# One-core graph-and-expert network: the last stage's weight ring takes over six shared buffers, and the first two experts are ranked from two banks

## The chip, the cores and the metric

The kernel runs on one core of one Trainium2 chip. The metric is the device time in microseconds (us) of one execution, from the first to the last instruction with what lies around them. Three runs of the kernel before gave a median of 4235.73 us (4232.37 to 4238.52). All instants below are us from the start of the profiled span.

## The reference, cut to what matters

The network works on 512 nodes of 768 features (`x`, float32) and passes through four groups of layers, each a graph layer, a mixing layer and a feed-forward layer. All stages but the last are the same in both kernels. The last one, a mixture of experts, normalises `x` (mean and variance over the features), and then:

- scores each token for 16 experts: sigmoid of `x` times a gate matrix;
- each expert takes the 64 tokens with the highest scores (ties go to the token with the lower number), which needs the rank of each token's score among the 512 scores of that expert;
- a chosen token goes through its expert: `Wd(silu(Wg x) * (Wu x))` with 3,072 hidden units, is multiplied by its score and added to the token's row;
- a shared expert of 1,536 hidden units, of the same form, works on all tokens and is added too.

The output is `x` with these sums added, 512 x 768 float32.

## The kernel before, in words

A layer called Tile builds the program: each engine (PE, which multiplies matrices; VectorE, "DVE" in the profile; ACT, the scalar engine; GpSimd, "POOL"; SP, which issues transfers) has a queue of its own, in an order that the layer's scheduler decides. `issue_after(i)` makes the instructions under it stand behind the instruction `i` in that order. Waits between engines and for buffers come by themselves from what the instructions read and write. Where ACT and VectorE read the same bank of the accumulation memory (a tile `ps`, 128 x 512 float32; there are eight), the layer makes them wait for each other.

**Stage before the last.** `last_two` multiplies `x` with the weights of the mixing layer (`m3_wqkv`, `m3_wp`) beside a graph layer. Its weights, like those of all earlier stages, go through the pool `wp` of six buffers of 1,152 KB (`w`, `wk`, `wr`, line 257; SP issues the transfers). It ends, token block by token block (four of 128), with `norm1` (L401 to L405: statistics and reciprocal on VectorE, the root on ACT, the scaling on VectorE) and writes each normalised block to a table `f3_there` in memory outside the core. `to_fm` with a cut (L354, L249, L251) transposes the first three blocks into the tile `xnT`, which has features on the partitions, with copies alternately on VectorE and ACT, and then the last block, in two triples of chunks.

**The last stage, `ffn3`.** On entry it closes the stack `cw`, which frees the pools `wp` and `rowp`, and opens a ring of 13 buffers, `f3_w`. Its head is a chain:

- the gate (L341), two half copies (L1717 on VectorE, L1718 on ACT), a turn back to tokens (L333), the sigmoid (L1720);
- `first_rank` for the experts 0 and 1: PE spreads the expert's 512 scores over all partitions into one bank (four transposes, L354). For each of the four token blocks, ACT takes the sign of the difference to every other score and adds the signs up (L1735), and VectorE counts the equal scores with weights of one half (L1738). Both read the bank;
- L1897 and L1898 make ranks of these; `choose(0)` compares the ranks with 0 to 63 and gives one-hot rows `oh` (L1766); `fetch(0)` multiplies them by the token numbers on PE, sums and casts these on VectorE (L1777, L1779), and GpSimd gathers the 128 rows from `f3_there` (L1781); `turn(0)` transposes them (L354) to `xg`;
- beside this, by hand, PE gets `shared(0, 0)` behind the last sign, and `shared(0, 1)` behind the product of `fetch`. `shared(u, b)` is half of one of 12 units of the shared expert: six matmuls of 128 x 512 in the program (twelve in the trace, since float32 takes two), then Silu on ACT (L1827) or a product on VectorE (L1829). Its weights `sw` come by GpSimd's queue (L1820), six buffers.

Then come 64 steps: eight pairs of experts, eight slices of the hidden units each. A step is `up` (two experts side by side, 64 columns each: L1851; Silu L1854, product L1855) and `down` (L1867). Its weights are six ring buffers: two `f3_Wg`, two `f3_Wu`, two `f3_Wd`. The `up` of the next step is placed ahead of the `down` of this one. A table `beside` says what else goes along with each step: the ranks, choices and gathers of the next pair (`rank`, L1752 and L1755), `way` (the products `os` of one-hot rows and scores, L1798, turned), `back` (the sum into `x`, L410), and the rest of the 12 shared units, cut into pieces and spread evenly over the first 60 steps. The last block's sums are followed by the stores of the output.

Of the kernel before, what the change touches and what calls it, by code (L numbers as in the profile page):

```python
# [1 line left out]

# [1 line left out]

# [7 lines left out]
BF16 = mybir.dt.bfloat16  # L12
# [3 lines left out]
OP = mybir.AluOpType  # L16
# [4 lines left out]
P = 128  # L21
# [148 lines left out]
class Net:  # L170
    def __init__(self, ctx, tc, dram, at, out):
        self.tc, self.nc, self.d, self.at, self.out = tc, tc.nc, dram, at, out
        nc = self.nc
        self.cw = ExitStack()
        self.wp = self.cw.enter_context(tc.tile_pool(name="wp", bufs=6, side="right"))
        self.keep = ctx.enter_context(tc.tile_pool(name="keep", bufs=1))
        self.small = ctx.enter_context(tc.tile_pool(name="small", bufs=4))
        self.rowp = self.cw.enter_context(tc.tile_pool(name="rowp", bufs=2, side="right"))
        self.pp = ctx.enter_context(tc.tile_pool(name="pp", bufs=8, space=PSUM))
        self.dp = ctx.enter_context(tc.tile_pool(name="dp", bufs=1, space=DRAM))  # L180
        self.turn = 0
# [36 lines left out]
        nc.gpsimd.memset(self.big0, -BIG)  # L218
        self.wq1 = keep.tile([P, KC, 32], F32, name="wq1")
        self.gate = None  # L220
        self.lower = keep.tile([P, P], BF16, name="lower")

        self.number = keep.tile([P, NT, 2], BF16, name="number")
        for t in range(NT):
            nc.gpsimd.memset(self.number[:, t, 1:2], float(t * P))
# [37 lines left out]
            self.before -= 1  # L263
        return t

    def wk(self, ap):

        return self.w(ap).rearrange("p (k n) -> p k n", k=KC)

    def wr(self, ap, pool=None):  # L270

# [81 lines left out]
        k = in_.shape[0]  # L353
        self.nc.tensor.transpose(out, in_, self.ident[:k, :k])  # L354

    def to_fm(self, x, out, cut=0):

        if cut:
            ps = [self.ps() for _ in range(KC)]
            for t in range(cut // P):  # L360
                for f in range(KC):
                    self.tr(ps[f][:, t * P : (t + 1) * P], x[:, t, f * P : (f + 1) * P])
            for f in range(KC):
                self.copy(out[:, f, :cut], ps[f][:, :cut])
            for f in range(0, KC, 3):
                p = self.ps()
                for k in range(3):
                    self.tr(p[:, k * P : (k + 1) * P], x[:, NT - 1, (f + k) * P : (f + k + 1) * P])
                self.copy(out[:, f : f + 3, cut:], p[:, :HW].rearrange("p (k n) -> p k n", k=3))
            return  # L370
        ps = [self.ps() for _ in range(KC)]
        for t in range(NT):
            for f in range(KC):
                self.tr(ps[f][:, t * P : (t + 1) * P], x[:, t, f * P : (f + 1) * P])
        for f in range(KC):
            self.copy(out[:, f, :], ps[f])

    def to_tm(self, xT, done):

# [14 lines left out]
    def norm1(self, x, out, t):  # L394
# [10 lines left out]
        nc.vector.tensor_scalar(out[:, t, :], x[:, t, :], mv[:, 0:1], r, OP.subtract, OP.mult)  # L405

    def add_x(self, t, nb, p):

# [1272 lines left out]
        yield  # L1681
        add(*after)

    def ffn3(self, xnT, gate, there):

# [4 lines left out]
        with ExitStack() as c:  # L1690
# [1 line left out]
            one = c.enter_context(tc.tile_pool(name="f3_one", bufs=1))  # L1692
            sp = c.enter_context(tc.tile_pool(name="f3_s", bufs=6))

            self.cw.close()
            self.wp = c.enter_context(tc.tile_pool(name="f3_w", bufs=13))

            first = self.small.tile([P, 1], F32, name="r3")
            with self.tc.issue_after(self.root):
                nc.scalar.activation(first, self.eps, AF.Sigmoid)  # L1700
            io = one.tile([P, P], F32, name="io")
            nc.gpsimd.iota(io, pattern=[[1, P]], base=0, channel_multiplier=0, allow_small_or_imprecise_dtypes=True)
# [26 lines left out]
            def first_rank(e):  # L1729
                p = self.ps()  # L1730
                for t in range(NT):
                    self.tr(p[:, t * P : (t + 1) * P], sc[:, t, e : e + 1].to_broadcast([P, P]))
                for t in range(NT):
                    junk = one.tile([P, N], BF16, name="sign")
                    i = nc.scalar.activation(junk, p, AF.Sign, scale=BIGGER, bias=low[:, t, e : e + 1],  # L1735
                                             accum_out=signs[:, t, e : e + 1])
                    junk = one.tile([P, N], BF16, name="junk")
                    nc.vector.scalar_tensor_tensor(junk, p, sc[:, t, e : e + 1], side[:, (3 - t) * P : (7 - t) * P],  # L1738
                                                   OP.is_equal, OP.mult, accum_out=sides[:, t, e : e + 1])
                return i  # L1740

            def rank(e):

# [25 lines left out]
            rows = {}  # L1769

            def fetch(q):

# [6 lines left out]
                nc.vector.tensor_copy(who, sums)  # L1779
                rows[q] = two.tile([P, D], F32, name="rows", bufs=1)  # L1780
                nc.gpsimd.indirect_dma_start(out=rows[q], out_offset=None, in_=there,  # L1781
                                             in_offset=bass.IndirectOffsetOnAxis(ap=who, axis=0))
                return i

            def turn(q):
# [8 lines left out]
            def way(q):  # L1794

                oh = chosen[q][0]
                os = two.tile([P, NT, 2, CAP], F32, name="os", bufs=1)
                nc.vector.tensor_mul(os, oh, sc[:, :, 2 * q : 2 * q + 2, None].to_broadcast([P, NT, 2, CAP]))  # L1798
                ways[q] = two.tile([P, N], F32, name="ohT")
                p = self.ps()  # L1800
                for t in range(NT):
# [10 lines left out]

            hs = {}

            def shared(u, b):
                if b == 0:
                    hs[u] = [two.tile([P, N], F32, name="hs")]
                    for n in ("f3_sg", "f3_su", "f3_sd"):
# [2 lines left out]
                        hs[u].append(w)  # L1821
                p = self.ps()
                w = hs[u][1 + b].rearrange("p (k m) -> p k m", k=KC)
                i = self.acc(p, [(w[:, k, :], xnT[:, k, :]) for k in range(KC)])
                h = hs[u][0]
                if b == 0:
                    nc.scalar.activation(h, p, AF.Silu)  # L1827
                else:
                    nc.vector.tensor_mul(h, h, p)  # L1829
# [7 lines left out]


            def up_w(q, n):
                return [[self.wk(d[w][2 * q + a, n]) for a in range(2)] for w in ("f3_Wg", "f3_Wu")]  # L1840

            def down_w(q, n):
                return [self.wr(d["f3_Wd"][2 * q + a, n]) for a in range(2)]

            def up(q, n, ws):
                xg = chosen[q][1]
# [85 lines left out]
def tile_net(ctx, tc, dram, at, out, only=ALL):  # L1932
# [56 lines left out]
    with tc.tile_pool(name="f3_x", bufs=1) as last:  # L1989
# [4 lines left out]
        with tc.tile_pool(name="f3_n", bufs=1) as p2:  # L1994
# [1 line left out]
            net.moe("f2", AF.Silu, xn)  # L1996
            there = net.last_two(xn, xnT, xn)

            net.to_fm(xn, xnT, (NT - 1) * P)
        net.ffn3(xnT, gate, there)  # L2000


def build(arrays, at, only=ALL):
# [20 lines left out]
```

## Time and profile before

| what | us |
|---|---|
| median of three runs | 4235.73 |
| the profiled execution | 4235.37 |
| its span, first to last instruction | 4233.6 |
| PE busy in the span | 4092.9 (97%) |
| VectorE, ACT, GpSimd busy | 1295.3, 664.4, 274.2 |
| first transfer of the last stage's ring issued | 3111.48 |
| first matmul of an expert | 3143.44 |
| end of the last matmul of an expert | 4224.0 |

The granted clock of PE is 0.989 over the span (1 is full). The three kinds of ring weights are 384 transfers of 1,152 KB, and take a median of 14.6 to 14.7 us from issue to landing, since several are under way at once. In the profile's rows a line such as L1735 stands for the instruction's source line, `sign<-ps,low` for what it writes and reads, and a bracket for the idle time of its engine ahead of it and what ended it. The ends of matmuls are modelled; their starts are not.

### The profile page before, as it was taken

The page shows a single profiled execution, that of the slowest core. Times are in us where ns is not written, and L with a number is a line of the kernel's source. Part 1 is how long each engine was busy: PE and PEld are TensorE (multiplying, and loading weights), DVE is VectorE, ACT ScalarE, POOL GpSimd, SP SyncE. Part 2 cuts the span into 40 slices and gives each one's busy share as a digit, 9 for nine tenths or more (in the row PEclk, how much of TensorE's full clock was granted, in tenths as well). Part 3 has the DMA queues.
Part 4 walks back from the last instruction along what each step waited for, and adds up shares of the span by engine and source line. Part 5 has one row for each costly group of instructions (what it writes and reads, how often), then busy time and mean ns, then how long its engine had stood idle before and what let it go on. Part 6 is the DMA issues. An engine that isn't in the chain of part 4 may idle for free. (4 is left out here: it accounts for less than half of the span.)

```text
span 4233.6 us, 40102 instructions
## 1 busy us (share of the span) xinstructions
PE 4092.9 (97%) x16356; PEld 2094.4 (49%) x16356; DVE 1295.3 (31%) x3096; ACT 664.4 (16%) x1258; POOL 274.2 (6%) x325
## 2 busy tenths in 40 slices
PE   9989999999989999999999999989989999999999
PEld 3434555554455566755644444445654444444444
DVE  8871111112432135613220101034751222122211
ACT  1221200001312223511200000012620000000000
POOL 1120000001022010000000000021110000000000
PEclk9999999999999999999999999989999999999999
DMA  3111011111047112211211111064069999999998
GB/s 111 53 64 56 23 45 67 68 56 54 18 178 291 42 56 72 109 45 56 98 44 57 55 56 53 4 237 155 12 282 427 427 427 426 427 427 427 420 425 366
DMA packets 99549, 710.90 MB, mean 168 GB/s; under 512 B 12608, under 2 KB 12945, under 8 KB 29985
## 3 DMA queue, kind: packets, MB, share of 16 engines
q1 hardware_dynamic: 78064, 601.20, 35.2%
q0 software_dynamic: 16816, 95.80, 6.0%
q10 hardware_dynamic: 4480, 11.28, 0.7%
q8 instruction: 132, 2.16, 0.2%
q14 instruction: 57, 0.46, 0.0%
HBM read 685.68 MB, written 22.54 MB: 167 GB/s over the span
## 5 line engine op out<-in xcount | busy, mean ns | idle before, releaser
L1851 PE MATMUL ps<-w,xg 128*64 128x384 f32 x3072 | 567.1, 489 | 0.3 <-DVE xg L249 0.3
L1851 PEld LDWEIGHTS ps<-w,xg 128*64 128x64 f32 x3072 | 235.8, 137 | 287.0 <-issue 257.5
L1473 PE MATMUL ps<-aT,w 128*128 128x512 f32 x864 | 372.3, 592 | 0.0
L1867 PE MATMUL ps<-w,hT 128*64 128x384 f32 x1536 | 319.4, 490 | 3.4 <-ACT hT L251 1.9
L333 PE MATMUL ps<-xnT,w 128*128 128x512 f32 (+1 forms) x732 | 321.5, 596 | 0.2 <-ACT xnT L251 0.2
L1473 PEld LDWEIGHTS ps<-aT,w 128*128 128x128 f32 x864 | 164.4, 190 | 203.4 <-issue 202.1
L333 PE MATMUL ps<-w,xnT 128*128 128x384 f32 x672 | 221.6, 487 | 0.2 <-DVE xnT L249 0.2
L333 PEld LDWEIGHTS ps<-xnT,w 128*128 128x128 f32 (+1 forms) x732 | 134.3, 184 | 174.7 <-issue 171.1
L1867 PEld LDWEIGHTS ps<-w,hT 128*64 128x64 f32 x1536 | 131.8, 137 | 166.7 <-issue 137.1
L410 DVE TENSOR_TENSOR x<-x,ps 128x384 f32<-128x384 f32 x224 | 123.5, 553 | 262.7 <-PE ps L333 192.7
L333 PE MATMUL ps<-C,parts 128*128 128x512 bf16 x864 | 188.6, 380 | 2.7 <-DVE inv L1495 2.7
L333 PE MATMUL ps<-w,hT 128*128 128x384 f32 x552 | 184.7, 490 | 3.9 <-ACTq L942 3.9
L514 PE MATMUL ps<-ohd,so 128*128 128x512 bf16 x816 | 184.1, 386 | 2.7 <-DVE so L511 2.7
L333 PEld LDWEIGHTS ps<-w,xnT 128*128 128x128 f32 x672 | 127.2, 190 | 88.4 <-issue 4.7
L1483 DVE TENSOR_TENSOR aT<-inv,ps 128x512 f32<-128x512 f32 x72 | 49.5, 687 | 365.6 <-PE ps L333 365.6
L1854 ACT ACTIVATE h<-ps 128x384 f32<-128x384 f32 x64 | 31.4, 490 | 781.5 <-PE ps L1851 781.5
L1855 DVE TENSOR_TENSOR h<-h,ps 128x384 f32<-128x384 f32 x64 | 35.4, 554 | 371.6 <-PE ps L1851 371.6
L333 PEld LDWEIGHTS ps<-w,hT 128*128 128x128 f32 x552 | 103.3, 190 | 81.2 <-ACT xbT L251 7.6
L333 PE MATMUL ps<-w,aT 128*128 128x384 f32 (+1 forms) x416 | 139.6, 486 | 0.5 <-DVE aT L249 0.4
L333 PE MATMUL ps<-xnT,sw 128*128 128x512 f32 x288 | 139.3, 615 | 0.0
L333 PEld LDWEIGHTS <-parts 128*128 128x128 bf16 x864 | 84.7, 98 | 108.1 <-issue 8.8
L514 PEld LDWEIGHTS <-so 128*128 128x128 bf16 x816 | 79.7, 99 | 107.6 <-DVE so L511 14.3
(511 smaller groups left out, 4826.7 us busy)
## 6 DMA issues: line engine op xcount, KB each, us to landing
w<-in_f_Wg_dram SPq DMA_DIRECT2D x128, 1152.0 KB, 14.6
w<-in_f_Wu_dram SPq DMA_DIRECT2D x128, 1152.0 KB, 14.7
w<-in_f_Wd_dram SPq DMA_DIRECT2D x128, 1152.0 KB, 14.6
w<-in_g_w_dram SPq DMA_DIRECT2D x54, 1152.0 KB, 5.1
w<-in_m_wqkv_dram SPq DMA_DIRECT2D x24, 1152.0 KB, 8.3
w<-in_g_t_dram SPq DMA_DIRECT2D x12, 1152.0 KB, 6.3
w<-in_m_wp_dram SPq DMA_DIRECT2D x8, 1152.0 KB, 5.2
ea<-in_edge_attr_dram SPq DMA_DIRECT2D x34, 256.0 KB, 2.7
```

What stands on the lines that cost most here:

```text
L333: i = self.nc.tensor.matmul(out, a, b, start=n == 0, stop=n == len(pairs) - 1)
L410: self.nc.vector.tensor_add(xs, xs, p)
L514: nc.tensor.matmul(p, so[:, n, t * P : (t + 1) * P], ohd[:, j, :], start=False, stop=j == (g + 1) * HJ - 1)
L1473: nc.tensor.matmul(outs[nb * 3 + f], w[:, k, f * P : (f + 1) * P], xT[:, k, :], start=first and k == 0, stop=last and k == KC - 1)
L1483: nc.vector.tensor_mul(aT[:, f, :], inv[:, r, :], p)
L1851: nc.tensor.matmul(p[a * 64 : a * 64 + 64, :HW], xg[:, k, a * CAP : (a + 1) * CAP], ws[b][a][:, k, :], start=k == 0, stop=k == KC - 1)
L1854: nc.scalar.activation(h, pg[:, :HW], AF.Silu)
L1855: nc.vector.tensor_mul(h, h, pu[:, :HW])
L1867: nc.tensor.matmul(po[nb][a * 64 : a * 64 + 64, :HW], hT[:, f * P + a * 64 : f * P + a * 64 + 64], wd[a][:, f, nb * HW : (nb + 1) * HW], s ...
```

## The change

- Pools: `rowp` gets a stack of its own. On entry, `ffn3` closes that stack only, keeps the six buffers of `wp`, and opens seven more (`f3_w`). The ring of the last stage goes through the six and then the seven, in turn.
- The copies into `xnT` for the last stage (`to_fm_last`): ACT takes the chunks 0, 1, 3 and 4 and the first triple of the last block, VectorE the chunks 2 and 5, issued behind the last scaling, and the second triple. The sigmoid's table is loaded behind ACT's last copy, not behind the last root.
- `first_ranks`: both experts' scores are spread, each in its own bank. ACT takes the signs of expert 0 while VectorE counts for expert 1; then they change over. Each engine has the same eight instructions as before.
- The product `os` of `way(q)` is issued behind the cast in `fetch(q)` (`casts[q]`).
- PE's order by hand: `shared(0, 0)`, the first three chunks of `shared(0, 1)`, the product of `fetch(0)`, the other three chunks, `shared(1, 0)`, and then `turn(0)`. The piece `shared(1, 0)` leaves the table `beside`.

```diff
-        self.rowp = self.cw.enter_context(tc.tile_pool(name="rowp", bufs=2, side="right"))
+        self.cr = ExitStack()
+        self.rowp = self.cr.enter_context(tc.tile_pool(name="rowp", bufs=2, side="right"))
...
+    def to_fm_last(self, x, out):
...
+        for f in (0, 1, 3, 4):
+            i = nc.scalar.copy(out[:, f, :cut], ps[f][:, :cut])
+        with self.tc.issue_after(self.scaled):
+            for f in (2, 5):
+                nc.vector.tensor_copy(out[:, f, :cut], ps[f][:, :cut])
...
+            if f:
+                nc.vector.tensor_copy(*at)
+            else:
+                with self.tc.issue_after(i.ins):
+                    i = nc.scalar.copy(*at)
+        return i.ins
...
-            self.cw.close()
-            self.wp = c.enter_context(tc.tile_pool(name="f3_w", bufs=13))
+            self.cr.close()
+            c.callback(self.cw.close)
+            more = c.enter_context(tc.tile_pool(name="f3_w", bufs=7))
+            self.taken = 0
+
+            def ring():
+                self.taken += 1
+                return self.wp if (self.taken - 1) % 13 < 6 else more
...
-            with self.tc.issue_after(self.root):
+            with self.tc.issue_after(turned):
                 nc.scalar.activation(first, self.eps, AF.Sigmoid)
...
+            def first_ranks():
+
+                ps = [self.ps() for _ in range(2)]
+                for e in range(2):
+                    for t in range(NT):
+                        self.tr(ps[e][:, t * P : (t + 1) * P], sc[:, t, e : e + 1].to_broadcast([P, P]))
+                for e in range(2):
+                    for t in range(NT):
+                        junk = one.tile([P, N], BF16, name="sign")
+                        i = nc.scalar.activation(junk, ps[e], AF.Sign, scale=BIGGER, bias=low[:, t, e : e + 1],
+                                                 accum_out=signs[:, t, e : e + 1])
+                    for t in range(NT):
+                        junk = one.tile([P, N], BF16, name="junk")
+                        j = nc.vector.scalar_tensor_tensor(
+                            junk, ps[1 - e], sc[:, t, 1 - e : 2 - e], side[:, (3 - t) * P : (7 - t) * P],
+                            OP.is_equal, OP.mult, accum_out=sides[:, t, 1 - e : 2 - e])
+                return i, j
...
-                nc.vector.tensor_mul(os, oh, sc[:, :, 2 * q : 2 * q + 2, None].to_broadcast([P, NT, 2, CAP]))
+                with tc.issue_after(casts[q]):
+                    nc.vector.tensor_mul(os, oh, sc[:, :, 2 * q : 2 * q + 2, None].to_broadcast([P, NT, 2, CAP]))
...
-                i = self.acc(p, [(w[:, k, :], xnT[:, k, :]) for k in range(KC)])
                 h = hs[u][0]
+                i = None
+                for k in range(KC):
+                    with tc.issue_after(i.ins) if i else nullcontext():
+                        i = nc.tensor.matmul(p, w[:, k, :], xnT[:, k, :], start=k == 0, stop=k == KC - 1)
+                    if between and k == KC // 2 - 1:
+                        with tc.issue_after(i.ins):
+                            i = between()
...
-                return [[self.wk(d[w][2 * q + a, n]) for a in range(2)] for w in ("f3_Wg", "f3_Wu")]
+                return [[self.wk(d[w][2 * q + a, n], ring()) for a in range(2)] for w in ("f3_Wg", "f3_Wu")]
...
-            rest = pieces[2:]
+            rest = pieces[2:4] + pieces[5:]
...
-            for e in range(2):
-                last = first_rank(e)
+            last, _ = first_ranks()
...
             with tc.issue_after(last.ins):
                 last = shared(0, 0)
             choose(0)
-
             with tc.issue_after(last.ins):
-                last = fetch(0)
+                last = shared(0, 1, lambda: fetch(0))
             with tc.issue_after(last.ins):
-                shared(0, 1)
+                shared(1, 0)
             turn(0)
```

More of the change, by code (lines that the diff above doesn't have):

```diff
@@ L1 @@
-from contextlib import ExitStack
+from contextlib import ExitStack, nullcontext
 import numpy as np
@@ L264, in w, with wk @@
         return t
-    def wk(self, ap):
-        return self.w(ap).rearrange("p (k n) -> p k n", k=KC)
+    def wk(self, ap, pool=None):
+        return self.w(ap, pool).rearrange("p (k n) -> p k n", k=KC)
     def wr(self, ap, pool=None):
@@ L354, in tr, with to_fm @@
         self.nc.tensor.transpose(out, in_, self.ident[:k, :k])
[L356 to L370, printed above, removed]
+    def to_fm(self, x, out):
         ps = [self.ps() for _ in range(KC)]
@@ L376, in to_fm @@
             self.copy(out[:, f, :], ps[f])
+    def to_fm_last(self, x, out):
+        nc, cut = self.nc, (NT - 1) * P
+        ps = [self.ps() for _ in range(KC)]
+        for t in range(NT - 1):
+            for f in range(KC):
+                self.tr(ps[f][:, t * P : (t + 1) * P], x[:, t, f * P : (f + 1) * P])
+        for f in (0, 1, 3, 4):
[3 more added lines that the diff above has]
+                nc.vector.tensor_copy(out[:, f, :cut], ps[f][:, :cut])
+        for f in range(0, KC, 3):
+            p = self.ps()
+            for k in range(3):
+                self.tr(p[:, k * P : (k + 1) * P], x[:, NT - 1, (f + k) * P : (f + k + 1) * P])
+            at = out[:, f : f + 3, cut:], p[:, :HW].rearrange("p (k n) -> p k n", k=3)
+            if f:
[4 more added lines that the diff above has]
+        return i.ins
     def to_tm(self, xT, done):
@@ L404, in norm1 @@
         nc.vector.reciprocal(r, r)
-        nc.vector.tensor_scalar(out[:, t, :], x[:, t, :], mv[:, 0:1], r, OP.subtract, OP.mult)
+        self.scaled = nc.vector.tensor_scalar(out[:, t, :], x[:, t, :], mv[:, 0:1], r, OP.subtract, OP.mult).ins
     def add_x(self, t, nb, p):
@@ L1682, in gnn3, with ffn3 @@
         add(*after)
-    def ffn3(self, xnT, gate, there):
+    def ffn3(self, xnT, gate, there, turned):
         nc, tc, d = self.nc, self.tc, self.d
@@ L1727, in ffn3 @@
             sides = one.tile([P, NT, 2], F32, name="sides")
[L1729 to L1740, printed above, removed]
+            def first_ranks():
[14 more added lines that the diff above has]
+                return i, j
             def rank(e):
@@ L1767, in choose @@
                                             above[:, t, 2 * q : 2 * q + 2, None].to_broadcast([P, 2, CAP]), OP.is_equal)
-            rows = {}
+            rows, casts = {}, {}
             def fetch(q):
@@ L1778, in fetch @@
                 who = two.tile([P, 1], I32, name="who")
-                nc.vector.tensor_copy(who, sums)
+                cast = nc.vector.tensor_copy(who, sums)
                 rows[q] = two.tile([P, D], F32, name="rows", bufs=1)
@@ L1782, in fetch @@
                                              in_offset=bass.IndirectOffsetOnAxis(ap=who, axis=0))
+                casts[q] = cast.ins
                 return i
@@ L1813, in ffn3, with shared @@
             hs = {}
-            def shared(u, b):
+            def shared(u, b, between=None):
                 if b == 0:
@@ L1839, in up_w @@
             def up_w(q, n):
-                return [[self.wk(d[w][2 * q + a, n]) for a in range(2)] for w in ("f3_Wg", "f3_Wu")]
+                return [[self.wk(d[w][2 * q + a, n], ring()) for a in range(2)] for w in ("f3_Wg", "f3_Wu")]
             def down_w(q, n):
-                return [self.wr(d["f3_Wd"][2 * q + a, n]) for a in range(2)]
+                return [self.wr(d["f3_Wd"][2 * q + a, n], ring()) for a in range(2)]
             def up(q, n, ws):
@@ L1997, in tile_net @@
             there = net.last_two(xn, xnT, xn)
-            net.to_fm(xn, xnT, (NT - 1) * P)
-        net.ffn3(xnT, gate, there)
+            turned = net.to_fm_last(xn, xnT)
+        net.ffn3(xnT, gate, there, turned)
 def build(arrays, at, only=ALL):
```

## The prediction

> **What bounds the kernel now.** The change touches only the last stage, so the first view is the table of busy time by stretch of that stage (columns: the stretch, its length, then busy us and instructions of PE, PE's weight loads, VectorE, ACT, GpSimd, then granted clock, DMA share, GB/s).
> ```profile
> 3100.00:3150.00 50.00, 39.41 (x165) 20.55 (x165) 17.76 (x46) 13.25 (x30) 5.60 (x11) 0.90 0.80 326
> ...
> 3300.00:3400.00 100.00, 100.00 (x487) 43.79 (x484) 16.99 (x41) 5.24 (x11) 3.16 (x5) 1.00 1.01 427
> ...
> 4100.00:4200.00 100.00, 99.38 (x531) 44.09 (x529) 15.68 (x28) 5.92 (x12) 0.00 (x0) 1.00 1.01 422
> ```
> From 3150 to the end PE and the DMA engines are both full: 427 GB/s in stretch after stretch, and PE without a hole. Only the 50 us at the stage's head have PE time to give. So I next split that head:
> ```profile
> 3126.00:3133.20 7.20, 0.00 (x0) 0.00 (x1) 4.41 (x14) 4.61 (x11) 0.54 (x1) 0.68 1.01 428
> 3133.20:3139.00 5.80, 5.74 (x10) 2.52 (x11) 1.45 (x6) 0.43 (x1) 1.04 (x1) 0.51 1.01 429
> ```
> PE stands still for 7.2 us while the first two experts are ranked, and then runs at half clock. The timeline says why the ranking is slow:
> ```profile
> 3126.07 0.69 ACT L1735 ACTIVATE sign<-ps,low 128x512 bf16<-128x512 f32 x1
> 3126.08 0.75 DVE L1738 SCALAR_TENSOR_TENSOR junk<-ps,sc,side 128x512 bf16<-128x512 f32 x1 [0.85 <-ACT sign L1735]
> ...
> 3126.94 0.75 DVE L1738 SCALAR_TENSOR_TENSOR junk<-ps,sc,side 128x512 bf16<-128x512 f32 x1
> ...
> 3127.73 0.69 ACT L1735 ACTIVATE sign<-ps,low 128x512 bf16<-128x512 f32 x1 [0.88 <-DVE junk L1738]
> ...
> 3128.54 0.75 DVE L1738 SCALAR_TENSOR_TENSOR junk<-ps,sc,side 128x512 bf16<-128x512 f32 x1 [0.84 <-ACT sign L1735]
> ```
> ACT and VectorE take turns on one bank (waits of 0.85 us at every step). Only at 3126.07, where one is in expert 0's bank and the other already in expert 1's, do they run at once, and neither gets longer. Last, the waits from 3160 to the end decide between PE and DMA:
> ```profile
> PEld ps L1867 <- DMA w<-in_f_Wg_dram: 10.4, 18, 0.8
> ...
> PEld ps L1851 <- DMA w<-in_f_Wd_dram: 7.5, 14, 0.8
> ```
> In 1,074 us PE is put down as waiting for weights for 18.7 us (0.8 for Wu), never over 0.8 at once; a gap of 0.6 to 0.8 also stands ("issue") at other changes between 64 and 128 columns, so hardly any of it is a real wait. Counting the weights' packets, a weight lands 12 to 24 us before its first matmul in mid-stage. The lead melts only in steps 61 to 63, where PE has no other work (12.2 us a step), and the last pair of Wd lands 2.0 us before its use. So PE sets the end, with the DMA 2 us behind it.
>
> **The change, part by part.** Sums are against the profiled execution: span 4233.6, own time 4235.37 (1.8 lie around the span), 0.4 under the median 4235.73.
>
> Transposed copies. In the trace before, the reciprocal waits behind a copy on VectorE: ACT's root ends at 3113.16, the scaling starts at 3113.86; without the copy it starts 0.24 us after the root (as at 3097.01 to 3097.25), 0.46 earlier. The sigmoid table (1.28 us) no longer stands ahead of ACT's copies; it moves into ACT's wait for the gate. VectorE keeps three copies of 0.55 behind the scaling and ends about where it did (3115.7), but the gate's matmuls no longer wait for ACT at 3116.2. Value 0.4, bounds 0 and 0.8.
>
> Ranks. Before: first sign 3120.37 to the sum's start 3132.43, 12.06 us. After, each engine has the same eight instructions, four in each bank, with one swap: ACT's pitch without waits is 0.81 (3125.26 to 3126.07), VectorE's 0.86 (3126.08 to 3126.94). 8 x 0.86 = 6.9, and 0.2 for starting on the second bank and the swap: 7.1. Gain 5.0; bounds 4.0 and 5.3 (0 if two banks don't help, a rival).
>
> The multiplication `os` (0.69 us, 3133.77) stands ahead of the sum that gives the row numbers; moved behind the cast, it frees 0.3.
>
> PE's order. Matmuls of the shared experts cost 0.44 each at full clock (12 in 5.3 us). Shared (0,0) ends at 3125.5, three chunks of (0,1) at 3128.2. The one-hot rows are due at 3128.1 (3133.74 less 5.4 and a little), so PE waits some 0.5 at the row numbers where it waited 7.3. Behind this wait stand the other half of (0,1) (2.65) and shared (1,0) (5.3): from 3129.0 they end at 3136.9. The gather is issued at 3135.00 - 0.4 - 5.0 - 0.3 + 0.4 (PE's part) = 3129.7 and lands 7.2 later, 3136.9, so they are hidden under it just as it ends. The first expert matmul came 1.2 us after the landing; I put it at 3138.2, against 3143.44: 5.2 earlier. Bounds 4.0 and 6.0.
>
> The stream behind. PE has 5.3 us of shared (1,0) less to do. I added up, in PE's order of the changed program, the distances from one matmul's start to the next by kind of pair as the trace has them (each kind repeats to 0.01 us): 1085.4 us before, which is the trace, and 1079.8 after, 5.6 less, since a few changes of width go too. Waits for `h` directly ahead of its use stay at six. PE's gain: 5.2 + 5.6 = 10.8.
>
> Ring. SP's queue now has four weights that wait only for buffers read before 3068, when the DMA engines are idle (99 GB/s from 3075, 1 before), a fifth at 3107; from the seventh on they wait, as all did, for the pools at 3111. Nothing stands behind these waits on SP but further weights. Cost 0 on PE: the stretch 2990 to 3075 has PE at full clock and no other loads. But the ring has 13 buffers either way. Nine weights from 3108, with gather and shared weights, are 28 us of transfer: the ring is full near 3137 and the DMA idles until PE gives back the first pair, 4.0 us into the first matmuls: 3142.2. The fourteenth weight is issued then and, with the 4.9 us that the first weight of the burst took from issue to landing, lands at 3147.1. Before, it queued behind the burst and landed at 3156.5. The transfers' gain is thus 9.4, not the 11 of four prefetched weights; with 2.0 in hand they allow 11.4.
>
> [...] The starts of the matmuls (no hole, weights landed a step ahead) say PE, 10.8. [...]
>
> **The rivals.**
> 1. Both shift as worked out: 4235.73 - 10.8 = 4225.0 (4222.5 to 4227.3). Chance 0.70.
> 2. Transfers become the bound: PE's lead in the last steps was 2.0 us, and restarting from an idle DMA costs more than the burst showed, or the rate dips (the stretch 4100 to 4200 has 422, not 427). For it: PE gains 1.4 more than the DMA. Against: some dips are PE's own, from a full ring. Gain 6 to 8.5: 4228.5. Chance 0.13.
> 3. The change does not do what it says: two banks do not let both engines run, and the ranks take 12 us as before. Then PE waits 5 us in the middle of shared (0,1). [...] in the trace 7.2 us cost the clock, 0.85 us a matmul for some 5 us. [...] by the trace's 5.8 us of slow stretch about 1. Gain 1.5 to 5: 4232. Against it: the pair at 3126.07. Chance 0.13.
> 4. Slower: transfers into the six shared buffers run slower than into the other seven, all stage long. The transfers gain 11.4, their margin included; the change loses from 11.4 us of added transfer on, 1.1% of the 1,062 us after the fourteenth weight, or 2.3% on each transfer into the six. [...] For it: only that PE has no reserve against the DMA. Against it: these buffers took all earlier weights, whose 9,216-byte packets took a median of 347 ns, as in the last stage, and between 2805 and 2825 came at 417 to 427 GB/s. Chance 0.04.
>
> **How the numbers follow.** Predicted is the first case, 4225.0. The range reaches down for a first expert matmul at 3137 with both terms at their good bounds (4221.5) and up through most of case 2 and a part of case 3 (4230.5). Apart from no change one can tell about 0.2%, 8.5 us, a time under 4227.3. Case 1 lies nearly all below it, with a little of case 2: faster 0.70; same takes the rest of 1 to 3, 0.26; slower 0.04.
>
> **What would show it.** Right: ACT's signs and VectorE's counts at pitches of 0.8 and 0.9 side by side, the last near 3127; no half clock after 3126; the gather issued near 3129.7; first expert matmul near 3138; DMA idle for some 5 us before 3142; four weights issued before 3075; PE without holes in the last three steps. Wrong: waits of PE for weights over 1 us in the last steps (case 2), the alternation still there (case 3), under 420 GB/s in mid-stage (case 4), or a first matmul held up by the copy of `xg`, which now stands behind a second Silu on ACT.

## The result, and the profile after

| | kernel before | changed kernel | ratio, 95% interval |
|---|---|---|---|
| median, 12 runs of each | 4235.92 us (4232.37 to 4238.52) | 4225.77 us (4223.38 to 4229.38) | 0.9976 (0.9968 to 0.9984) |
| the same again on another chip, 41 and 13 runs | 4234.88 us (4232.66 to 4241.63) | 4226.66 us (4224.06 to 4230.08) | 0.998 (0.9972 to 0.9989) |
| the profiled execution | 4235.37 us | 4225.14 us | |
| its span | 4233.6 us | 4223.3 us | |

The change gains 10.2 us in the first comparison and 8.2 in the second; 10.8 was forecast. The profiled executions differ by several us ahead of the last stage already, where the kernels hardly differ (the last scaling lies between 3111.6 and 3117.2 in all of them), so from here on I count from the start of the last scaling of `norm1` (3113.86 before, 3112.49 after), which cuts that part off.

| us after the last scaling | before | after | earlier |
|---|---|---|---|
| first sign | 6.5 | 6.4 | 0.1 |
| the ranks' sum starts | 18.8 | 13.7 | 5.1 |
| gather issued | 21.1 | 15.7 | 5.4 |
| first matmul of an expert | 29.6 | 24.6 | 5.0 |
| 14th weight landed | 42.6 | 33.3 | 9.3 |
| last weight landed | 1103.5 | 1096.8 | 6.7 |
| end of the span | 1119.7 | 1110.8 | 8.9 |

A weight has landed when its last packet is written. The last two rows hold what the forecast missed: the transfers are 9.3 us early at the 14th weight, and only 6.7 at the last one. A second trace of the changed kernel, taken for the second line of the first table, has 33.4, 1097.9 and 1112.0 in the last three rows, so differences between traces here are good to about 1 us. First the views. The changed kernel's busy time by stretch (columns as in the forecast):
```profile
3120.00:3126.00 6.00, 6.00 (x15) 2.66 (x14) 5.57 (x17) 5.25 (x15) 0.54 (x1) 1.00 1.00 422
3126.00:3133.20 7.20, 7.15 (x21) 3.26 (x20) 2.78 (x10) 1.81 (x2) 1.79 (x2) 1.00 1.02 432
3139.00:3143.50 4.50, 4.50 (x30) 2.42 (x28) 0.00 (x0) 0.49 (x1) 0.00 (x0) 1.00 0.42 122
3300.00:3400.00 100.00, 100.00 (x528) 44.54 (x526) 15.31 (x34) 5.55 (x11) 2.63 (x4) 1.00 1.01 425
...
4100.00:4200.00 100.00, 97.38 (x530) 42.97 (x530) 13.99 (x25) 5.44 (x11) 0.00 (x0) 1.00 1.01 423
```
In the second row PE is busy for 7.15 us where it stood still for 7.2, and the clock is whole. The third row is the forecast hole in the transfers: 122 GB/s near 3141, the ring being full. The last two rows are the surprise: in mid-stage 425 GB/s, not 427, with the DMA just as full (1.01), and between 4100 and 4200 PE loses 2.0 us more (97.38 against 99.38).

The timeline shows the ranks side by side:
```profile
3119.45 0.75 DVE L1762 SCALAR_TENSOR_TENSOR junk<-ps,sc,side 128x512 bf16<-128x512 f32 x1 [1.05 <-PE ps L355]
3119.74 0.69 ACT L1758 ACTIVATE sign<-ps,low 128x512 bf16<-128x512 f32 x1
3120.24 0.75 DVE L1762 SCALAR_TENSOR_TENSOR junk<-ps,sc,side 128x512 bf16<-128x512 f32 x1
3120.55 0.69 ACT L1758 ACTIVATE sign<-ps,low 128x512 bf16<-128x512 f32 x1
```
Both engines run at pitches of 0.8 us, each at its old length: two banks work as the one overlapping pair of the trace before promised. PE's head in the changed kernel:
```profile
3126.89 0.60 PE L334 MATMUL ps<-number,oh 128*128 128x2 bf16 x4
3127.35 7.97 PE L1855 MATMUL ps<-xnT,sw 128*128 128x512 f32 x18
3135.88 0.85 PE L355 MATMUL ps<-ident,rows 128*128 128x128 f32 x6 [0.56 <-DMA rows<-f_there,who]
3137.10 7.96 PE L1884 MATMUL ps<-w,xg 128*64 128x384 f32 x48 [0.37 <-issue]
```
Eighteen shared matmuls (7.97 us) cover the gather and end 0.56 us before it lands. The end, though, has changed hands. The chain of waits of the changed kernel, its end (us, length, what):
```profile
4166.95 20.49 DMA w<-in_f_Wd_dram
...
4187.50 22.15 DMA w<-in_f_Wd_dram
...
4209.69 4.08 PE ps L1900 x20
4213.78 5.37 PE ps L334 x16
```
and PE's timeline of the last 30 us, where the brackets are its waits:
```profile
4193.01 4.09 PE L1884 MATMUL ps<-w,xg 128*64 128x384 f32 x24 [0.98 <-DMA w<-in_f_Wg_dram]
...
4198.60 3.76 PE L1884 MATMUL ps<-w,xg 128*64 128x384 f32 x21 [1.02 <-DMA w<-in_f_Wu_dram]
...
4204.18 4.35 PE L1900 MATMUL ps<-w,hT 128*64 128x384 f32 x24 [0.23 <-DMA w<-in_f_Wd_dram]
4209.69 4.08 PE L1900 MATMUL ps<-w,hT 128*64 128x384 f32 x20 [1.16 <-DMA w<-in_f_Wd_dram]
```
Before, the chain's last 80 us held no transfer:
```profile
by line: PE ps L1851 44.4%; PE ps L1867 31.0%; PE ps L333 9.1%; PE ps L354 3.3%; DVE h L1855 0.6%; DVE x L410 0.6%; issue 0.2%; DVEq L1855 0.0%
```
Now PE waits four times for weights, 3.4 us in all. My theory: the gain stops where the transfers become the bound, and they lost part of their head start because they run slower. The rival: PE's shorter work sets the end, and what is missing lies in the head.

### The profile page after: what moved, and what is told of

Read it like the earlier page. It is cut to its first block, busy times and chain, and to the rows that moved or that the text cites. A ratio compares the mean times of both kernels' runs of the same rounds, so it can differ in the third digit from the quotient of the medians.

```text
span 4223.3 us, 40102 instructions
## 1 busy us (share of the span) xinstructions
PE 4084.5 (97%) x16356; PEld 2083.0 (49%) x16356; DVE 1293.0 (31%) x3095; ACT 664.6 (16%) x1259; POOL 274.0 (6%) x325
## 5 line engine op out<-in xcount | busy, mean ns | idle before, releaser
L523 DVE TENSOR_SCALAR so<-io,ind,worth 128x256 bf16<-128x256 int16 x408 | 122.2, 355 | 35.4 <-PE ps L526 35.2
```

Of the source, the lines that this page charges most:

```text
L523: made["so"] = nc.vector.tensor_scalar(so[:, n, :], io[:, h * 256 : (h + 1) * 256], ind[:, 0, j : j + 1], worth[:, n, j : j + 1], OP.is_eq ...
```

## Experiments: one part at a time

**The ring alone** (kernel before; the lines that hand the pool on are cut):
```diff
...
-            self.cw.close()
-            self.wp = c.enter_context(tc.tile_pool(name="f3_w", bufs=13))
+            self.cr.close()
+            c.callback(self.cw.close)
+            more = c.enter_context(tc.tile_pool(name="f3_w", bufs=7))
...
+                return self.wp if (self.taken - 1) % 13 < 6 else more
...
```


> The kernel before with the new ring alone (six shared buffers and seven more); ranks, copies and PE's order as before. My theory: PE sets the end and starts the experts at 3143.4 as before, so nothing is gained, 4236; the transfers get 4 us ahead (first pair given back at 3147.4, fourteenth weight landed near 3152.4 instead of 3156.5), which only widens the last weights' lead from 2 to about 6 us. The rival, that the transfers alone set the end: about 4 us faster, 4232.

Measured: 4233.62 us, kernel before on the same chip 4234.82; ratio 0.9997 (0.9989 to 1.0005). The chain over the last 80 us has no transfer:
```profile
by line: PE ps L1858 44.0%; PE ps L1874 30.2%; PE ps L334 9.1%; PE ps L355 3.3%; DVE h L1862 0.6%; DVE x L411 0.6%; issue 0.2%; DVEq L1862 0.0%
```
Weights that land earlier are worth nothing that shows while PE sets the end (the interval includes 1). And this kernel, whose 14th weight lands 4.7 us earlier than before (37.9 us after the scaling), gets its last one 0.2 us later (1103.7). In part that can be PE, which gives the buffers back no earlier; but between 3300 and 3400 its transfers run at 425 GB/s, as in the changed kernel, against 427 before. The slower rate comes with the new ring.

**All but the ring** (changed kernel):
```diff
-            c.callback(self.cw.close)
-            more = c.enter_context(tc.tile_pool(name="f3_w", bufs=7))
+            self.cw.close()
+            self.wp = c.enter_context(tc.tile_pool(name="f3_w", bufs=13))
...
-                return self.wp if (self.taken - 1) % 13 < 6 else more
+                return self.wp
```


> The changed kernel with the old ring: 13 buffers of one pool, all waiting for the pools at 3111; ranks, copies and PE's order as changed. My theory: PE starts the experts near 3137 but the burst of 13 weights still ends near 3154, so the transfers are where they were, and PE can use only the 2 us that it had as lead at the end, perhaps 2 more from fuller transfers in mid-stage: 4232 to 4234, with waits for weights in the last three steps. The rival, that PE alone counts: the whole gain, 4225 to 4226.

Measured: 4230.98 us, ratio 0.9991 (0.9983 to 0.9999). The head is as early as in the changed kernel (ranks 13.7, first expert 24.9 us after the scaling), the 14th weight lands at 43.9, and the chain over the last 80 us is transfers:
```profile
by line: DMA w<-in_f_Wd_dram 48.7%; DMA w<-in_f_Wu_dram 20.3%; PE ps L334 7.4%; PE ps L1884 5.9%; PE ps L1900 4.5%; DVE x L422 0.6%; PE ps L355 0.5%; issue 0.2%; SPq L258 0.0%
```
The stage ends at 1117.1, 2.6 earlier than before. The two halves of the change bring 1.2 (not told from nothing) and 3.8 us one by one and 8 to 10 together: each takes away one of two bounds that lie close to each other.

**No third piece under the gather** (changed kernel, `shared(1, 0)` back in the table):
```diff
-            rest = pieces[2:4] + pieces[5:]
+            rest = pieces[2:]
...
-                last = shared(0, 1, lambda: fetch(0))
-            with tc.issue_after(last.ins):
-                shared(1, 0)
+                shared(0, 1, lambda: fetch(0))
```


> The changed kernel with shared (1,0) back in the table of later steps. First expert matmul as in the changed kernel (3137), transfers too, but PE has 5.6 us more to do behind it. If PE then sets the end: 6.3 us faster than before, 4229.6. If the transfers set the end as they do in the changed kernel: no difference to it, 4225.8.

Measured: 4230.45 us, ratio 0.999 (0.9981 to 0.9998), and PE alone in the end of the chain:
```profile
by line: PE ps L1884 43.8%; PE ps L1900 26.3%; PE ps L334 7.4%; PE ps L355 3.3%; DVE h L1888 0.6%; DVE x L422 0.6%; issue 0.2%; DVEq L1888 0.0%
```
The 5.3 us of shared matmuls came back as 4.7 us in the stage (1115.5 against 1110.8). Not all of this is the work itself. PE now stands while the gather is under way, and works slowly behind it:
```profile
3135.21 1.54 PE L355 MATMUL ps<-ident,rows 128*128 128x128 f32 x6 [5.69 <-DMA rows<-f_there,who]
3136.76 5.41 PE L1884 MATMUL ps<-w,xg 128*64 128x384 f32 x22
```
The granted clock is half for 6.8 us here, and the first pairs of expert matmuls start 0.63 us apart, where the changed kernel has 0.32. That costs some 1.6 us. So the third piece fills the gather and also keeps the clock whole.

**One bank for both engines** (changed kernel; both work on expert 0's bank, then on expert 1's):
```diff
-                    for t in range(NT):
                         junk = one.tile([P, N], BF16, name="junk")
                         j = nc.vector.scalar_tensor_tensor(
-                            junk, ps[1 - e], sc[:, t, 1 - e : 2 - e], side[:, (3 - t) * P : (7 - t) * P],
-                            OP.is_equal, OP.mult, accum_out=sides[:, t, 1 - e : 2 - e])
+                            junk, ps[e], sc[:, t, e : e + 1], side[:, (3 - t) * P : (7 - t) * P],
+                            OP.is_equal, OP.mult, accum_out=sides[:, t, e : e + 1])
```


> The changed kernel, but ACT and VectorE rank the same expert in turns on the same bank, as before; all else as changed. The ranks take 12 us instead of 7: the first expert matmul comes 5.0 us later than in the changed kernel (3142.1), and PE and transfers both move with it: 4230.8. If PE's gap of about 5 us in the middle of shared (0,1) halves its clock, the 18 matmuls behind it take up to 8 us longer and the first expert matmul comes at 3145 to 3150: 4234 to 4239. If the ranks were not what delayed the first expert: 4225.8.

Measured: 4233.34 us, ratio 0.9997 (0.9988 to 1.0005). Ranks at 18.7 us after the scaling, as in the kernel before. Its timeline, to be held against PE's head above:
```profile
3134.88 0.75 PE L334 MATMUL ps<-number,oh 128*128 128x2 bf16 x4 [4.74 <-issue]
3135.48 11.01 PE L1854 MATMUL ps<-xnT,sw 128*128 128x512 f32 x18
```
PE stands for 4.74 us, and then the same 18 matmuls take 11.01 us instead of 7.97, because the granted clock is half for 6.8 us. The twelve matmuls behind the gap of the kernel before had paid the same way (5.3 us at full clock):
```profile
3133.84 7.90 PE L333 MATMUL ps<-xnT,sw 128*128 128x512 f32 x12
```
The first expert comes 7.3 us later than in the changed kernel: 5.0 by the ranks, and 2.3 more between the gather's issue and the first expert (11.2 against 8.9). This is the forecast's third rival, built: without the two banks nothing is left of the gain at the head.

## Experiments: which bound, and how far off

**17.7 us less of PE, in both kernels.** Units 10 and 11 of the shared expert use one of six chunks in gate and up; nothing else is left out, all loads stay. First the edit of the changed kernel, then that of the kernel before:
```diff
-                for k in range(KC):
+                n = 1 if u >= 10 else KC
+                for k in range(n):
                     with tc.issue_after(i.ins) if i else nullcontext():
-                        i = nc.tensor.matmul(p, w[:, k, :], xnT[:, k, :], start=k == 0, stop=k == KC - 1)
+                        i = nc.tensor.matmul(p, w[:, k, :], xnT[:, k, :], start=k == 0, stop=k == n - 1)
...
-                i = self.acc(p, [(w[:, k, :], xnT[:, k, :]) for k in range(KC)])
+                i = self.acc(p, [(w[:, k, :], xnT[:, k, :]) for k in range(1 if u >= 10 else KC)])
```


> The changed kernel with work left out on TensorE alone: units 10 and 11 of the shared expert use one of the six chunks in their gate and up matmuls (20 matmuls of 128x512 fewer in each unit's pair; loads, order and all other work are kept), 17.7 us of TensorE in the middle of the stage. Theory, that the changed kernel's transfers set the end: next to nothing of it comes out, 0 to 1 us: 4224.8 to 4225.8. Rival, that TensorE's work sets the end: 17.7 us less, about 4208.

> The kernel before with the same work left out on TensorE alone (units 10 and 11 of the shared expert use one of six chunks in gate and up), 17.7 us of TensorE. It measures what the transfers of the kernel before had in hand: the time falls only until they set the end. By the forecast's figure of 2.0 us in hand: 4232.9. By the trace, in which its transfers also pause for full buffers by some 1 to 2 us late in the stage: up to 4.5 us faster, 4230.4. Rival, that TensorE alone sets the end and transfers are far behind it: 17.7 us less, 4217.

Measured, beside 4234.88 for the kernel before and 4226.66 for the changed one on the same chip: the changed kernel with less work 4225.64, the kernel before with less work 4231.98. Of 17.7 us, 1.0 and 2.9 come out. The chain over the last 80 us of the latter shows who took over:
```profile
by line: DMA w<-in_f_Wd_dram 49.4%; DMA w<-in_f_Wu_dram 24.7%; PE ps L333 6.0%; PE ps L1867 4.5%; DVE x L410 0.6%; issue 0.2%; SPq L257 0.0%
```
So the transfers of the kernel before had 2.9 us in hand (forecast: 2.0), and those of the changed kernel 1.0 at most. By the medians alone the 2.9 is not told from nothing (ratio 0.9993, 0.9984 to 1.0001), but the ends of the stage agree: 1116.9 here and 1117.1 with the old ring above, against 1119.7, is the floor of the old ring's transfers, 1110.6 (changed kernel with less work) that of the new ring, and the changed kernel stands on it with 1110.8. The rival falls.

**Fourteen buffers** (changed kernel; paid for by two of six buffers of the shared expert's weights and one of two `outs`):
```diff
-            sp = c.enter_context(tc.tile_pool(name="f3_s", bufs=6))
+            sp = c.enter_context(tc.tile_pool(name="f3_s", bufs=4))
...
-            more = c.enter_context(tc.tile_pool(name="f3_w", bufs=7))
+            more = c.enter_context(tc.tile_pool(name="f3_w", bufs=8))
...
-                return self.wp if (self.taken - 1) % 13 < 6 else more
+                return self.wp if (self.taken - 1) % 14 < 6 else more
...
-                    outs[q] = two.tile([P, D], F32, name="outs")
+                    outs[q] = two.tile([P, D], F32, name="outs", bufs=1)
```


> The changed kernel with one buffer more in its ring (fourteen: the six shared ones and eight more; room is made by four instead of six buffers for the sums of the shared expert's gate and one instead of two for the rows sent back). Theory, that the changed kernel ends a little behind its transfers (TensorE waits some 1.7 us for the last weights): one transfer more is in flight when the ring is full, so the last weight comes up to 2.8 us earlier against the work, TensorE waits for no weight in the last steps, and the median is about 1.7 us under the changed kernel's, 4224.1 against 4225.8, with TensorE alone in the end of the chain of waits. Rival, that TensorE's work alone sets the end: 4225.8, as the changed kernel.

Measured: 4225.09 us (kernel before 4234.88), ratio 0.9977 (0.9969 to 0.9984): no gain that shows. The expectation called the pool of six one for sums; it holds the shared weights `sw`, and that spoilt the test. With four buffers, two of them (2 x 393,216 bytes, 1.85 us at 425 GB/s) no longer arrive ahead of the last scaling but inside the stage: in the 100 us ahead of it, GpSimd's queue moves 2.75 MB instead of 3.54. The last weight comes 0.7 us earlier, not 2.8. By itself this run decides nothing.

## Experiments: why the transfers slowed

The 9,216-byte packets of the weights in mid-stage, worked out from the trace's packet records: in the kernel before 0.7% of them take more than 347 ns, in the changed kernel 20.7% (the slowest hundredth 358 ns and more). By place in the ring the slow ones cluster at five or six neighbouring places of thirteen. The compiled programs show what sets the six shared buffers apart: on each partition they start at byte 174,048 and every 9,216 bytes on, which is 32 bytes past a multiple of 64; the pool `f3_w` starts at a multiple of 512.

**The six moved to multiples of 512** (changed kernel, 480 bytes left empty above them), and **the seven moved off by 32 bytes** (changed kernel):
```diff
+        self.edge = self.cw.enter_context(tc.tile_pool(name="edge", bufs=1, side="right")).tile([P, 120], F32, name="edge")
         self.wp = self.cw.enter_context(tc.tile_pool(name="wp", bufs=6, side="right"))
```
```diff
+            off = c.enter_context(tc.tile_pool(name="f3_off", bufs=1)).tile([P, 8], F32, name="off")
             more = c.enter_context(tc.tile_pool(name="f3_w", bufs=7))
```


> The changed kernel with 480 bytes left empty at the upper edge of SBUF, so that the six shared buffers, which in both kernels begin 32 bytes past a multiple of 64, begin at multiples of 512 bytes, as the seven others do. Theory, that the start address is what makes packets into the shared buffers take 349 to 354 ns instead of 347: all thirteen places of the ring show 347 ns, the mean step from one weight's landing to the next falls from 2.874 to about 2.866 us, the last weight lands about 3 us earlier after the last scaling (1094 instead of 1096.8 us), TensorE's last waits go, and the median is some 1.7 us under the changed kernel's: 4224.1. Rival, that it is the place of these buffers or the order of the ring and not the start address: packets stay at 349 to 354 ns, and the time at 4225.8.

> The changed kernel with its seven further buffers moved up by 32 bytes, so that all thirteen begin 32 bytes past a multiple of 64. Theory of the start address: packets of nearly all places of the ring show 349 to 354 ns, the mean step from landing to landing grows from 2.874 to about 2.883 us, the last weight lands about 3.5 us later after the last scaling (1100 us), and since the transfers set the end already, the median grows by as much: about 4229. Rival, that place or order is the cause: the seven stay at 347 ns and the time at 4225.8.

| | packets over 347 ns | landing to landing, us | last weight, us after scaling | end, us after scaling | median, us |
|---|---|---|---|---|---|
| all thirteen at multiples of 512 | 0.6% | 2.865 | 1093.5 | 1107.6 | 4222.88 |
| changed kernel, six off by 32 | 20.7% | 2.874 | 1096.8 | 1110.8 | 4225.77, 4226.66 |
| all thirteen off by 32 | 89.8% | 2.906 | 1108.6 | 1122.7 | 4237.21 |

The same stretch of the aligned kernel, and of the one with all off:
```profile
3300.00:3400.00 100.00, 100.00 (x516) 44.69 (x518) 18.47 (x44) 5.56 (x11) 2.64 (x4) 1.00 1.01 427
```
```profile
3300.00:3400.00 100.00, 100.00 (x518) 44.64 (x518) 18.46 (x44) 5.55 (x11) 2.63 (x4) 1.00 1.01 421
```
427, 425, 421 GB/s, with a DMA that is full in all three; the share cannot tell, the rate can. The issues show it too (the last figure of each row is the median us from issue to landing), first the changed kernel, then aligned, then all off:
```profile
w<-in_f_Wd_dram SPq DMA_DIRECT2D x128, 1152.0 KB, 17.4
```
```profile
w<-in_f_Wd_dram SPq DMA_DIRECT2D x128, 1152.0 KB, 15.9
```
```profile
w<-in_f_Wd_dram SPq DMA_DIRECT2D x128, 1152.0 KB, 22.3
```
The direction was as expected both times, so the start address is the cause and not the place or the order of the ring; the size of the second was three times the expected one (11.8 us, not 3.5). With all thirteen off, the whole gain is gone: the stage ends 3.0 us later than before in the trace, and the ratio to the kernel before is 1.0006 (0.9998 to 1.0014). The aligned kernel has 0.9972 (0.9961 to 0.9982), 12.0 us. That interval overlaps the changed kernel's, so what it gains over the changed kernel's 10.2 and 8.2 rests on the last weight (3.3 us earlier than in the first trace of the changed kernel, 4.4 than in the second) and on the opposite run more than on the medians. PE's last wait in it shrinks but does not vanish:
```profile
4205.58 4.14 PE L1901 MATMUL ps<-w,hT 128*64 128x384 f32 x24
4210.37 4.08 PE L1901 MATMUL ps<-w,hT 128*64 128x384 f32 x20 [0.65 <-DMA w<-in_f_Wd_dram]
```

**Controls.** The changed kernel once more (its times are in the first table), and the kernel before with the 480 bytes:

> The changed kernel once more, unaltered, so that it stands on the same chip as the aligned kernel before, and for the size of what the alignment of the changed kernel brought (4222.88 us, on a chip where the kernel before took 4234.88). Theory of start addresses and transfers that set the end: 1.5 to 3.3 us above the aligned one's ratio, that is 4224.5 to 4226. Rival, that the aligned kernel's 2.9 us were a difference between chips: a ratio to the kernel before of 0.9972, as the aligned one has.

> The kernel before with 480 bytes left empty at the upper edge of SBUF, so that its six shared buffers start at multiples of 512 bytes. Its last stage does not use these six, and its thirteen others start at multiples of 512 bytes already. Theory, that start addresses matter only where transfers set the end, which is the last stage of the changed kernel: no difference, within 1 us of the kernel before. Rival, that earlier stages gain from the alignment too and so explain part of what the aligned changed kernel gained: 1.5 us or more faster than the kernel before, with the last scaling as much earlier.

The kernel before with the 480 bytes takes 4234.14 us beside 4234.88, ratio 0.9999 (0.9991 to 1.0008): where the ring does not use the six, their address is worth nothing that shows. Its packets do show it: of the 14,592 packets of 9,216 bytes that SP's queue brings to the six in the earlier stages, 10.0% take 348 to 360 ns in the kernel before, and 1.1% here. So the trace before held the sign already, and it needs no new ring. The changed kernel's 0.998 lies above the aligned one's 0.9972 by 3.4 us, a little more than the theory's 1.5 to 3.3.

**Aligned and fourteen buffers:**

> Both together: the changed kernel with fourteen buffers and with the six shared ones at multiples of 512 bytes. Theory: either edit alone lets TensorE's work set the end again, so both together bring no more than one: about 4224.1 (the transfers then have some 4 us in hand, which shows as weights that land earlier before their use, not as time). Rival, that the transfers still set the end with either edit: the gains add, about 4222.

4221.33 us, ratio 0.9969 (0.9958 to 0.998): the fastest of all, 1.5 us under the aligned one, which the intervals do not tell apart; it has the flaw of the other run with fourteen too. In its last 75 us PE waits 0.3 us for a weight.

## Why the prediction held, and which term was off

- **Head.** Ranks: forecast 5.0 earlier, measured 5.1. Gather issued 5.4 earlier. First expert 5.2 earlier by the forecast, 0.4 of it ahead of the scaling; measured 5.0 from the scaling on, and ahead of it 0.5 (the scaling starts 0.23 us behind the end of ACT's root, not 0.70). Each step is in the profile where it was forecast.
- **Half clock and third rival.** The forecast put the delay of the first expert from 18 matmuls behind a gap of some 5 us at about 1 us, by the 5.8 us of slow stretch in the trace before; that the rival's gain could go down to 1.5 was the author's estimate and not shown there. With one bank, a gap of 4.74 us did cost the clock (half for 6.8 us); the 18 matmuls took 3.0 longer (11.01 against 7.97) and the first expert came 2.3 later. The 1 was too low for the trace before as well, whose twelve took 7.90, not 5.3. The rival's 4232 stands beside 4233.3.
- **PE's stream.** Forecast 5.6 less. From the first expert's matmul to the end the kernel before takes 1090.1 us; in the aligned kernel with fourteen buffers, where PE hardly waits for a weight, it is 1082.0: 8.1 less. Waiting for weights is none of the difference: behind the first expert's matmul the trace before has five gaps of PE over 0.15 us, 3.35 in all, each for a transposed `hT`, and the other kernel has five with 3.24. The ring alone shortens the stretch by 0.8 (1089.3), which is mostly one of these five that falls away (0.74). Why the forecast's sum came 2.5 short stays open.
- **Transfers: the term that was off.** The forecast read: "The transfers' gain is thus 9.4 [...]; with 2.0 in hand they allow 11.4." The 9.4, which has the 0.4 ahead of the scaling in it, measured 9.3 from the scaling on (9.8 with the 0.5 ahead); the 2.0 measured 2.9. What was put at nothing is the slower rate: against the aligned kernel, 370 landings x (2.8741 - 2.8653) = 3.3 us. They allow 9.3 + 2.9 - 3.3 = 8.9, and the stage is 8.9 shorter. With the 0.5 ahead of the scaling that is 9.3 after rounding, against 10.2 and 8.2 in the medians. The second trace of the changed kernel bears the sum out: with a step of 2.8771 it loses 4.4 us; 9.2 + 2.9 - 4.4 = 7.7 are allowed, and its stage is 7.8 shorter.
- **The fourth rival had the right mechanism.** It was argued down with a median packet of 347 ns for earlier weights in the same buffers. The median could not show it: with a fifth of the packets longer, it is still 347. The forecast's sign for it, under 420 GB/s in mid-stage, was set too low as well: 425 here, and 421 even with all off. The rival's point of decision was right. With all off, the loss is 370 x (2.9056 - 2.8653) = 14.9; 14.9 - 9.3 - 2.9 = 2.7 slower than before, and the stage is 3.0 slower.
- **PE as the bound before.** The ring alone brought nothing that shows, so in the kernel before PE was the bound, with the DMA 2.9 us behind. The forecast's 9.4 for the transfers alone is nearer to the traces' 9.3 than its 10.8 is, but by chance, since it leaves out the 2.9 in hand and the 3.3 lost.

The forecast took the smaller of two terms, 10.8 for PE and 11.4 for the transfers, what is gained ahead of the scaling included. Measured in the same way, PE could give about 13 (the stage of the aligned kernel with fourteen buffers is 12.6 shorter) and the transfers 9.3. So the smaller term was the other one: the transfers set the end, and the last waits of 1.02 and 1.16 us are the forecast's own sign of its second rival. That 4225.0 is only 0.8 and 1.7 us off is luck in this part: what the transfers lost happened to leave them close to the 10.8. The head, and that PE and transfers lie close to each other, were foreseen rightly.

## What to carry to other kernels

Where PE and the transfers are both full, work out both sums, and take the smaller: a gain on one is worth only what the other has in hand (here 1.2 and 3.8 us one by one, 8 to 10 together). Measure that reserve by leaving out work on one engine. Before a pool's buffers are put into a stream that has no reserve, look at their start addresses, and judge a rate by the GB/s of a stretch and by the tail of the packets, not by a DMA share or a median: here the share was 1.01 at 427, 425 and 421 GB/s, and the median packet 347 ns with none of the thirteen off and with six.

## What the runs showed of the hardware

- A start address in SBUF, the core's own memory, that was 32 bytes past a multiple of 64 slowed packets of 9,216 bytes on their way in: their mean in mid-stage was 348.0 ns with none of thirteen buffers off, 348.9 (0.3% more) with six and 352.8 (1.4% more) with all. Only such starts and multiples of 512 were tried. The six start 480 bytes past a multiple of 512 and the seven, when moved, 32; with all off the means lie at 352 to 353 ns at every place of the ring, so both starts cost the same. The loss grew faster than the number of such buffers: six cost 3.3 us (4.4 in the second trace), all thirteen 14.9. Why was not tried.
- PE's clock: with 7.2 us of standing, half clock for 10.2 us, from 2.7 us after the start of the gap (kernel before); with 5.7 us, for 6.8 (no third piece); with 4.74 us, for 6.8 (one bank).
- ACT and VectorE on two banks: at pitches of 0.8 us side by side, neither's instruction longer than alone (0.69 and 0.75).
